# A graph layer with residual and layer norm: normalisation in steps of one block, the first x on another queue, and two planned times

## The chip, the cores and the metric

The kernel runs on one core of a Trainium2 chip. The metric is the device time of one execution in microseconds (us); lower is better. The engines have short names in the profile: PE is TensorE (matrix products), PEld its weight loads, DVE is VectorE, ACT is ScalarE, POOL is GpSimd, SP is SyncE. A name with a q (SPq, ACTq) is the engine's instruction queue, as when it issues a DMA.

## The reference, cut to what matters

There are 6250 nodes with 128 features each, and 100000 edges sorted by their target. Each edge takes the source node's features through one of two linear maps, by its type; the results are summed at the target. A third linear map of the node itself is added, then ReLU, the residual and a layer norm without weights.

```python
Xs = X[src]
m_data = Xs @ W_data.T + b_data
m_ctrl = Xs @ W_control.T + b_control
msg = jnp.where((edge_types == 0)[:, None], m_data, m_ctrl)
agg = jax.ops.segment_sum(msg, dst, num_segments=X.shape[0])
out = agg + (X @ W_self.T + b_self)
...
x = _layernorm(x + relu(out))
```

## The kernel before, in words

The nodes are padded to 49 blocks of 128. The work has two stages.

*Building the messages.* Both maps are linear, so they are applied to the nodes and not to the edges. Step y (L462, L464) multiplies a block of x by W_data and W_control side by side and adds the bias, in float32 in PSUM. The steps yh, y1, ym, y2 and yl cut the result into three bfloat16 parts that add up to it: ACT copies one part out (L473) and PE subtracts it (L480), twice over, and then ACT copies the last. The parts stand in SBUF (m, or m3) and are stored in DRAM as a table. x comes transposed in seven pieces (PARTS: 4 blocks, then 8 at a time) by `load_x`, from ACT's queue. The bias is cut in three in the same way at the very start, by DVE (L271 to L274), and ACT copies its parts into a bfloat16 tile (L276) that the second product of y reads.

*Summing over the edges.* For 35 of the blocks, in seven groups of five, PE fetches the messages by products with 0/1 matrices. While the table is still being built, a group's edges are read in windows (`starts`, one DMA for each block from SP's queue) and sorted into slots (fields, hot, tri, rank, rest, two, v). Where the windows begin is found at the start: r0, one target of every 200 edges, is loaded; DVE compares it (begun, L280); PE counts (L284); POOL fetches one row of edges for each block (er, L290); DVE counts within it; PE turns the result (step "turned", L355); and DVE writes the starts (step "first", L357), which SP reads to issue the windows. Then each block goes through 25 rounds of three steps: g, where PE picks 128 message rows into PSUM (L756, tile g_ps, four buffers); e, where ACT copies them to SBUF as bfloat16 (L771, tile gs, eight buffers; the 25th goes to "mixed"; DVE helps in the last group alone); and s, where PE adds them into the block's sum (L232, agg). Once in a block there is step o: x times W_self and its bias are added to the same sum, with the same helper `by_columns` (L232, agg<-w_sb). The other 14 blocks take their messages from the table by indirect DMAs that POOL issues (msg), and PE sums them (step gm, agg_g).

*Finishing.* When a block's sum is complete, DVE adds its three parts (step whole), adds the residual after the ReLU, and takes mean and variance (step sum). For five blocks together (four in the last, for the final group four and one) `normalise` computes scale and shift (root, rooted, scale), and `apply` has ACT apply them: one instruction of 128x128 at L190 for each block, in place. Then the rows are stored (step out).

*What sets the order.* The order of instructions on each engine is fixed when the program is built, by a planner, `Order`. Each stream of work yields steps with a name, a planned time on an engine, and the steps that it needs. `Order.run` keeps a planned clock for each engine (`free`), and for each step the time at which it can start: when the steps that it needs have ended plus 0.25 us (AFTER). It takes the engine on which something can start first, and among that engine's steps that can start within 0.1 us of that (CLOSE) the one with the smallest due time. The due times are written out in `due`: for a round of block b, 76 + 13.1 x (b + round/25), and 1 more for its copy e; for the normalisation of groups, 76 + 10 + 13.1 x the number of blocks up to the group's end; for y, LEAD plus its block times a pace. Planned times do not change what an instruction does; they decide where it stands in its engine's queue. At run time each engine works its queue in that order, and waits at an instruction whose inputs or buffers are not ready.

Of the kernel before, what the change touches and what calls it, by code (L numbers as in the profile page):

```python
# [9 lines left out]
F32 = mybir.dt.float32  # L10
BF16 = mybir.dt.bfloat16
I32 = mybir.dt.int32
AF = mybir.ActivationFunctionType
# [6 lines left out]
P = 128  # L20
D = 128
D3 = 3 * D
# [86 lines left out]
@with_exitstack  # L109
def kernel(  # L110
    ctx: ExitStack,
    tc: tile.TileContext,
    x: bass.AP,
    xt: bass.AP,
    edges: bass.AP,
    w: bass.AP,
    bias: bass.AP,
    out: bass.AP,
):

    nc = tc.nc  # L140
    dram = ctx.enter_context(tc.tile_pool(name="dram", bufs=1, space=DRAM))
    const = ctx.enter_context(tc.tile_pool(name="const", bufs=1))
    table = dram.tile([NT * P, D3], BF16, name="table")
    packed = dram.tile([NPB, NT * R], BF16, name="packed")
    total = const.tile([1, 1], I32, name="total")

    def finish(h, agg, xs):

        nc.vector.scalar_tensor_tensor(h, agg, 0.0, xs, op0=ALU.max, op1=ALU.add)

    def add_parts(agg, work):
        whole = work.tile([P, D], F32, name="whole")
        nc.vector.tensor_reduce(whole, agg.rearrange("p (i c) -> p c i", i=3), axis=AX.X, op=ALU.add)  # L153
        return whole

    def load_rows(b, work, name="xs", bufs=2):
        xs = work.tile([P, D], F32, name=name, bufs=bufs)
        nc.sync.dma_start(xs, x[b * P : (b + 1) * P, :])
        return xs

    def stats(mv, h, work):
        st = work.tile([P, 6], F32, name="st")
        nc.vector.bn_stats(st, h)
        nc.vector.bn_aggr(mv, st)

    def root(mv, n, work):
        v = work.tile([P, Q], F32, name="v")
        nc.vector.tensor_scalar_add(v[:, :n], mv[:, :n, 1], EPS)
        s0 = work.tile([P, Q], F32, name="s0")
        nc.scalar.activation(s0[:, :n], v[:, :n], AF.Sqrt)  # L170
        return v, s0

    def scale(mv, v, s0, n, work):

        r0 = work.tile([P, Q], F32, name="r0")
        nc.vector.reciprocal(r0[:, :n], s0[:, :n])
        q = work.tile([P, Q], F32, name="q")
        nc.vector.tensor_mul(q[:, :n], v[:, :n], r0[:, :n])
        nc.vector.tensor_add(q[:, :n], q[:, :n], s0[:, :n])
        rstd = work.tile([P, Q], F32, name="rstd")  # L180
        nc.vector.reciprocal(rstd[:, :n], q[:, :n])
        nc.vector.tensor_scalar_mul(rstd[:, :n], rstd[:, :n], 2.0)
        shift = work.tile([P, Q], F32, name="shift")
        nc.vector.scalar_tensor_tensor(shift[:, :n], mv[:, :n, 0], -1.0, rstd[:, :n],
                                       op0=ALU.mult, op1=ALU.mult)
        return rstd, shift

    def apply(h, rstd, shift, n):
        for j in range(n):
            nc.scalar.activation(h[:, j, :], h[:, j, :], AF.Identity,  # L190
                                 bias=shift[:, j : j + 1], scale=rstd[:, j : j + 1])

    def store_out(h, b0, n, by=nc.sync):
        n0 = b0 * P
        full = min(n, (N - n0) // P)
        if full:
            by.dma_start(
                out[n0 : n0 + full * P, :].rearrange("(b p) f -> p b f", p=P), h[:, :full, :]
            )
        if full < n:  # L200
            n1 = n0 + full * P
            nc.sync.dma_start(out[n1:N, :], h[: N - n1, full, :])

    norm = stats, root, scale, apply, store_out

    with ExitStack() as main:
        sums_over_windows(main, tc, x, xt, edges, w, bias, table, packed, total,
                          add_parts, finish, load_rows, norm)

    matched = nc.values_load(total[0:1, 0:1])  # L210
    with tc.If(matched != E), ExitStack() as rest:
        sums_over_all(rest, tc, xt, edges, w, bias, table, dram, finish, load_rows, norm)


def sums_over_windows(ctx, tc, x, xt, edges, w, bias, table, packed, total,
# [21 lines left out]
    early = ctx.enter_context(ExitStack())  # L237
    build = early.enter_context(tc.tile_pool(name="build", bufs=2))
    ps_y = early.enter_context(tc.tile_pool(name="ps_y", bufs=YB, space=PSUM))
    b1 = build.tile([1, D3], F32, name="b1", bufs=1)  # L240
    A.dma_start(b1, bias)
    w_sb = const.tile([D, D3], F32, name="w_sb")
    A.dma_start(w_sb, w)


    iota_f = const.tile([P, 640], F32, name="iota_f")
# [46 lines left out]
        in_offset=bass.IndirectOffsetOnAxis(ap=row_i[:, 0:1], axis=0),  # L293
    )

    order.free.update(V=7.0, T=6.5, G=8.0)


    pid1 = const.tile([P, 1], F32, name="pid1")
# [74 lines left out]
            )  # L374


    xts, ys = {}, {}
    at_part = [sum(PARTS[:g]) for g in range(len(PARTS))]
    two_blocks = [(g, b, min(2, at_part[g] + n - b))
                  for g, n in enumerate(PARTS) for b in range(at_part[g], at_part[g] + n, 2)]  # L380


    LEAD, BUILT = 8.0, 76
    BLOCK = 13.1
    PACE = 1.68
    AHEAD, FIRST = 26.0, 20
# [60 lines left out]
    def load_x():  # L447
        for g, n in enumerate(PARTS):
            free = [("y", at_part[g - 1] - 1)] if g > 1 else []
            yield step(("xt", g), {"A": 0.45}, *free, lag=3.5)  # L450
            xts[g] = build.tile([D, max(PARTS), P], F32, name="xt")[:, :n]
            A.dma_start(xts[g].rearrange("p b c -> p (b c)"),
                        xt[:, at_part[g] * P : (at_part[g] + n) * P])

    def multiply():
        for i, (g, b, n) in enumerate(two_blocks):
            for j in range(n):
                free = [("yl", two_blocks[i - YB][1])] if i >= YB and j == 0 else []
                yield step(("y", b + j), {"T": 0.97}, ("xt", g), *free)
                if j == 0:  # L460
                    y = ys[b] = ps_y.tile([P, 2, 2 * D], F32, name="y")
                T.matmul(y[:, j, :], xts[g][:, b + j - at_part[g], :], w_sb[:, : 2 * D],  # L462
                         start=j == 0, stop=False, skip_group_check=True)
                T.matmul(y[:, j, :], ones_b, bias3[:, : 2 * D], start=False, stop=True, skip_group_check=True)  # L464
# [326 lines left out]
    def own_of(blocks, begun):  # L791

        for i, b in enumerate(blocks):
            yield step(("agg", b), {"S": 0.0}, *([("whole", blocks[i - 1])] if i else []))
            yield step(("o", b), {"T": 0.5}, ("xs", b), begun(b))
            by_columns(aggs[b][:, :D], x_ts.pop(b), w_sb[:, 2 * D :], start=False, stop=False,
                       skip_group_check=True)
            by_columns(aggs[b][:, :D], ones_b, bias3[:, 2 * D :], start=False, stop=False,
                       skip_group_check=True)
# [16 lines left out]
    def normalise(pieces, last):  # L816

        for grp, (get, b0, q0, n) in enumerate(pieces):
            yield step((last, "root", grp), {"V": 0.2}, ("sum", b0 + n - 1))
            h, mv = get()  # L820
            h, mv = h[:, q0 : q0 + n, :], mv[:, q0 : q0 + n, :]
            v, s0 = root(mv, n, work)
            yield step((last, "rooted", grp), {"A": 0.3}, (last, "root", grp))
            yield step((last, "scale", grp), {"V": 1.0}, (last, "rooted", grp))
            scales = scale(mv, v, s0, n, work)
            yield step((last, "apply", grp), {"A": 0.28 * n}, (last, "scale", grp))
            apply(h, *scales, n)
            at_end = last == "p" and grp == len(pieces) - 1
            yield step((last, "out", grp), {"A": 0.4} if at_end else {"S": 0.3}, (last, "apply", grp))
            store_out(h, b0, n, nc.scalar if at_end else nc.sync)  # L830


# [99 lines left out]
def sums_over_all(ctx, tc, xt, edges, w, bias, table, dram, finish, load_rows, norm):  # L932
# [69 lines left out]
    for b0 in range(0, NB, Q):  # L1002
        n = min(Q, NB - b0)
        h = work.tile([P, Q, D], F32, name="h")
        mv = work.tile([P, Q, 2], F32, name="mv")
        for j in range(n):
            s_in = work.tile([P, D], F32, name="s_in")
            nc.sync.dma_start(s_in, sums[(b0 + j) * P : (b0 + j + 1) * P, :])
            xt_b = work.tile([D, P], F32, name="xt_b")
            nc.sync.dma_start(xt_b, xt[:, (b0 + j) * P : (b0 + j + 1) * P])  # L1010
            own = ps.tile([P, D], F32, name="own")
            nc.tensor.matmul(own, xt_b, w_self, start=True, stop=False)
            nc.tensor.matmul(own, one, b_self, start=False, stop=True)
            nc.vector.tensor_add(s_in, s_in, own)
            finish(h[:, j, :], s_in, load_rows(b0 + j, work))
            stats(mv[:, j, :], h[:, j, :], work)
        v, s0 = root(mv, n, work)
        apply(h, *scale(mv, v, s0, n, work), n)
        store_out(h, b0, n)


# [29 lines left out]
```

## Time and profile before

| | |
|---|---|
| median of three timed runs | 545.55 us (544.28 to 546.70) |
| the profiled execution | 628.27 us, span 626.6 us |
| mean granted TensorE clock | 0.985 |
| copies of g_ps to SBUF (L771, ACT) | 804 of 494 ns, 337.2 us busy |
| picking products (L756, PE) | 3430, 330.8 us busy |
| normalising instructions (L190, ACT) | 35 of 497 ns and 14 of 488 ns |
| loads of x for y (L452) | 7 DMAs from ACT's queue, 256 to 512 KB |

The profiled execution is longer than the timed ones, so times read in its trace are compared with its own 628.27 us. A row of the timeline gives the start in us, the length in us, engine, line, operation, out<-in and the count; a row with a count above one merges instructions that follow each other, and its length is from the first start to the last end. What stands in brackets is how long the engine was idle before, and what ended that. A row of the chain of waits gives the start, the length and what the end of the program was then waiting for. Products on PE overlap, so the distance between starts says more than the length of one.

### The profile page before, as it was taken

The page shows a single profiled execution, that of the slowest core. Times are in us where ns is not written, and L with a number is a line of the kernel's source. Part 1 is how long each engine was busy: PE and PEld are TensorE (multiplying, and loading weights), DVE is VectorE, ACT ScalarE, POOL GpSimd, SP SyncE. Part 2 cuts the span into 40 slices and gives each one's busy share as a digit, 9 for nine tenths or more (in the row PEclk, how much of TensorE's full clock was granted, in tenths as well). Part 3 has the DMA queues.
Part 4 walks back from the last instruction along what each step waited for, and adds up shares of the span by engine and source line. Part 5 has one row for each costly group of instructions (what it writes and reads, how often), then busy time and mean ns, then how long its engine had stood idle before and what let it go on. Part 6 is the DMA issues. An engine that isn't in the chain of part 4 may idle for free.

```text
span 626.6 us, 26397 instructions
## 1 busy us (share of the span) xinstructions
PE 550.4 (88%) x11222; PEld 441.2 (70%) x11222; DVE 429.4 (69%) x962; ACT 424.7 (68%) x1008; POOL 292.8 (47%) x267
## 2 busy tenths in 40 slices
PE   5899888896989898897988989999999998888994
PEld 3555466675768686786877877788777787666783
DVE  4767677567667777776787766877686667446784
ACT  6755555565587666777767676786767876676684
POOL 1000026654465556655556464665646554554400
PEclk9999988999899999999999999999999999999998
DMA  3567754324243433435333433443344542534300
GB/s 108 168 196 221 249 188 128 117 66 158 58 127 123 127 111 117 136 109 152 93 128 114 142 122 106 127 144 106 122 133 119 157 152 68 161 103 146 106 18 27
DMA packets 60932, 79.19 MB, mean 126 GB/s; under 512 B 15760, under 2 KB 51371, under 8 KB 60807
## 3 DMA queue, kind: packets, MB, share of 16 engines
q1 hardware_dynamic: 47109, 48.88, 24.3%
q0 software_dynamic: 12400, 25.08, 14.3%
q10 hardware_dynamic: 1298, 3.48, 1.6%
q8 instruction: 89, 1.46, 0.9%
q14 instruction: 36, 0.29, 0.1%
HBM read 64.35 MB, written 13.05 MB: 124 GB/s over the span
## 4 chain that ended last, share of the span: by engine, by line
PE 80%; ACT 7%; issue 5%; DVE 4%; DMA 2%; SPq 1%; another core or an unknown queue 0%; POOL 0%; ACTq 0%; DVEq 0%; POOLq 0%
PE agg L232 27%; PE g_ps L756 26%; PE acc L232 8%; PE agg_g L232 8%; PE small L602 7%; ACT gs L771 5%; PE y L462 2%; ACT h_p L190 1%; DMA rows<-packed 1%; DVE slot L565 1%; PE y L480 1%; DVE hot_st L548 1%; ACT h_g L190 1%; PE y L464 0%; DMA xt<-in_xt 0%
## 5 line engine op out<-in xcount | busy, mean ns | idle before, releaser
L771 ACT CAST gs<-g_ps 128x384 bf16<-128x384 f32 x804 | 337.2, 494 | 151.3 <-PE g_ps L756 97.4
L857 POOL DMA_INDIRECT msg<-table,idx x252 | 283.1, 1124 | 208.0 <-PE g_ps L756 90.5
L756 PE MATMUL g_ps<-m,rows 128*32 128x384 bf16 x3430 | 330.8, 334 | 19.2 <-ACT gs L771 11.6
L232 PE MATMUL agg<-gs,hot_d 128*32 128x384 bf16 x3360 | 304.4, 338 | 27.8 <-ACT gs L771 12.9
L232 PEld LDWEIGHTS <-hot_d 128*32 128x32 bf16 x3500 | 198.9, 137 | 66.7 <-issue 56.4
L756 PEld LDWEIGHTS <-rows 128*32 128x32 bf16 x3430 | 185.5, 138 | 46.4 <-issue 40.6
L565 DVE TENSOR_REDUCE slot<-acc 128x5 bf16<-128x490 f32 x126 | 83.8, 665 | 75.5 <-PE acc L232 39.7
L232 PE MATMUL agg_g<-msg,hot_g 128*32 128x384 bf16 x1008 | 107.2, 330 | 1.2 <-issue 1.1
L741 DVE TENSOR_TENSOR hot_d<-count,to 128x1664 bf16<-128x1664 bf16 x70 | 74.7, 1068 | 21.7 <-PE agg L232 12.8
L602 PE MATMUL small<-hot_st,two 128*32 128x98 bf16 x1260 | 70.9, 290 | 1.4 <-issue 1.3
L602 PEld LDWEIGHTS <-two 128*32 128x32 bf16 x1260 | 56.8, 118 | 6.7 <-issue 4.6
L232 PE MATMUL acc<-hot_st,rest 128*32 128x490 bf16 x476 | 55.1, 380 | 6.1 <-DVE slot L565 5.0
L232 PE MATMUL acc<-hot_st,tri 128*32 128x490 bf16 x504 | 58.8, 376 | 1.0 <-DVE hot_st L548 0.9
L473 ACT CAST m<-y 128x512 bf16<-128x512 f32 (+1 forms) x75 | 40.6, 580 | 25.7 <-PE y L480 18.0
L232 PEld LDWEIGHTS <-hot_g 128*32 128x32 bf16 x1008 | 51.4, 125 | 4.9 <-issue 3.0
L548 DVE TENSOR_TENSOR hot_st<-count,st_b 128x2940 bf16<-128x2940 bf16 x21 | 41.9, 1997 | 13.7 <-PE small L602 5.4
L696 POOL DMA_INDIRECT mixed<-table,row_i x7 | 7.4, 1055 | 87.3 <-PE g_ps L756 81.2
L727 DVE TENSOR_SCALAR rows<-rows,pid 128x3136 bf16<-128x3136 bf16 x35 | 36.3, 1038 | 3.3 <-DMA rows<-packed 3.3
L153 DVE TENSOR_REDUCE whole<-agg 128x128 f32<-128x384 f32 x35 | 19.4, 553 | 27.5 <-PE g_ps L756 23.4
L462 PE MATMUL y<-w_sb,xt 128*128 128x256 f32 x98 | 31.6, 409 | 1.7 <-DMA xt<-in_xt 1.7
L232 PEld LDWEIGHTS <-rest 128*32 128x32 bf16 x476 | 20.9, 99 | 16.0 <-issue 15.3
L771 DVE CAST gs<-g_ps 128x384 bf16<-128x384 f32 x36 | 19.3, 554 | 13.7 <-PE g_ps L756 12.2
(140 smaller groups left out, 423.6 us busy)
## 6 DMA issues: line engine op xcount, KB each, us to landing
rows<-packed SPq DMA_DIRECT2D x35, 784.0 KB
table<-m SPq DMA_DIRECT2D x10, 768.0 KB
msg<-table,idx POOLq DMA_INDIRECT x252
xt<-in_xt ACTq DMA_DIRECT2D x5, 512.0 KB
xt_p<-in_xt SPq DMA_DIRECT2D x35, 64.0 KB
xs_p<-in_x SPq DMA_DIRECT2D x35, 64.0 KB
out<-h_p SPq DMA_DIRECT2D x6, 320.0 KB
table<-m SPq DMA_DIRECT2D x2, 480.0 KB
```

Of the source, the lines that this page charges most:

```text
L153: nc.vector.tensor_reduce(whole, agg.rearrange("p (i c) -> p c i", i=3), axis=AX.X, op=ALU.add)
L232: T.matmul(out[c : c + 32], lhsT[:, c : c + 32], rhs, **flags)
L462: T.matmul(y[:, j, :], xts[g][:, b + j - at_part[g], :], w_sb[:, : 2 * D], start=j == 0, stop=False, skip_group_check=True)
L473: A.copy(part_of(b, n, i), ys[b][:, :n, :].rearrange("p b (t c) -> p t b c", t=2))
L548: V.tensor_tensor(hot, counted[n][:, None, 1 : NT + 1, :].to_broadcast([P, KC, NT, n]), fields[grp][2][:, c * KC : c * KC + KC, None, :].t ...
L565: V.tensor_reduce(slots[grp][:, k, :], by_q, axis=AX.X, op=ALU.max)
L602: T.matmul(vt[c0 : c0 + R, q // 2, :], two[:, k % KC, i, :, q], hot[:, k % KC, :, q], start=k == 0 and q < 2, stop=k == KT - 1, skip_group ...
L727: V.tensor_scalar(rows[b], rows[b], pid1, None, op0=ALU.is_equal)
L741: V.tensor_tensor(hot, counted[DC][:, :, :n], places[grp][:, q, None, c * DC : c * DC + n].to_broadcast([P, P, n]), op=ALU.is_equal)
L756: T.matmul(g_ps[t * R : (t + 1) * R, :D3], rows[b][:, :, s], m3[:, s, :], start=True, stop=True)
L771: (A.copy if e == "A" else V.tensor_copy)(gs[at], g_tiles.pop((b, g))[at, :D3])
L857: G.indirect_dma_start(out=msgs[j, k], out_offset=None, in_=table[:, :], in_offset=bass.IndirectOffsetOnAxis(ap=idx[:, j, k : k + 1], axis=0),
```

## The change

The first load of x (4 blocks, 256 KB) is issued by SP, directly behind r0, in place of ACT. On ACT's queue the weights are now loaded ahead of the bias. The planner's starting clock for PE goes from 6.5 to 5.0 and LEAD, from which the due times of the building steps count, from 8 to 6. `apply` handles one block; in `normalise` each block's application is a planner step of its own of 0.39 us, where there was one step of 0.28 us times the number of blocks. The planned time of y goes from 0.97 to 1.0, that of o (x times W_self) from 0.5 to 0.25. The fallback path for inputs that the windows do not cover calls `apply` in a loop; it is not executed on these inputs.

```diff
-    def apply(h, rstd, shift, n):
-        for j in range(n):
-            nc.scalar.activation(h[:, j, :], h[:, j, :], AF.Identity,
-                                 bias=shift[:, j : j + 1], scale=rstd[:, j : j + 1])
+    def apply(h, rstd, shift, j):
+        nc.scalar.activation(h[:, j, :], h[:, j, :], AF.Identity,
+                             bias=shift[:, j : j + 1], scale=rstd[:, j : j + 1])
...
+    w_sb = const.tile([D, D3], F32, name="w_sb")
+    A.dma_start(w_sb, w)
+    xts = {0: build.tile([D, max(PARTS), P], F32, name="xt")[:, : PARTS[0]]}
+    nc.sync.dma_start(xts[0].rearrange("p b c -> p (b c)"), xt[:, : PARTS[0] * P])
     b1 = build.tile([1, D3], F32, name="b1", bufs=1)
     A.dma_start(b1, bias)
-    w_sb = const.tile([D, D3], F32, name="w_sb")
-    A.dma_start(w_sb, w)
...
-    order.free.update(V=7.0, T=6.5, G=8.0)
+    order.free.update(V=7.0, T=5.0, G=8.0)
...
-    LEAD, BUILT = 8.0, 76
+    LEAD, BUILT = 6.0, 76
...
-            yield step(("xt", g), {"A": 0.45}, *free, lag=3.5)
+            yield step(("xt", g), {"A": 0.45} if g else {"S": 0.0}, *free, lag=3.5 if g else 0.0)
+            if not g:
+                continue
...
-                yield step(("y", b + j), {"T": 0.97}, ("xt", g), *free)
+                yield step(("y", b + j), {"T": 1.0}, ("xt", g), *free)
...
-            yield step(("o", b), {"T": 0.5}, ("xs", b), begun(b))
+            yield step(("o", b), {"T": 0.25}, ("xs", b), begun(b))
...
-            yield step((last, "apply", grp), {"A": 0.28 * n}, (last, "scale", grp))
-            apply(h, *scales, n)
+            for j in range(n):
+                yield step((last, "apply", grp, j), {"A": 0.39}, (last, "scale", grp))
+                apply(h, *scales, j)
             at_end = last == "p" and grp == len(pieces) - 1
-            yield step((last, "out", grp), {"A": 0.4} if at_end else {"S": 0.3}, (last, "apply", grp))
+            yield step((last, "out", grp), {"A": 0.4} if at_end else {"S": 0.3}, (last, "apply", grp, n - 1))
```

More of the change, by code (lines that the diff above doesn't have):

```diff
@@ L374, in starts @@
             )
-    xts, ys = {}, {}
+    ys = {}
     at_part = [sum(PARTS[:g]) for g in range(len(PARTS))]
@@ L1017, in sums_over_all @@
         v, s0 = root(mv, n, work)
-        apply(h, *scale(mv, v, s0, n, work), n)
+        scales = scale(mv, v, s0, n, work)
+        for j in range(n):
+            apply(h, *scales, j)
         store_out(h, b0, n)
```

## The prediction

> **What bounds the kernel now.** I read the page first: the shares of the engines, then the chain that ended last.
>
> ```profile
> PE 550.4 (88%) x11222; PEld 441.2 (70%) x11222; DVE 429.4 (69%) x962; ACT 424.7 (68%) x1008; POOL 292.8 (47%) x267
> PE 80%; ACT 7%; issue 5%; DVE 4%; DMA 2%; SPq 1%; another core or an unknown queue 0%; POOL 0%; ACTq 0%; DVEq 0%; POOLq 0%
> ```
>
> TensorE (PE) is the bound: busy for 88% of the span, on 80% of the chain. ScalarE (ACT) is second, 7% of the chain although it is idle for a third of the time: PE waits for it in places, not on average. So an edit pays only where PE stands still. From the gaps between PE rows of the timeline from 100 to 617 us I count about 51 us of them.
>
> Next the chain of waits, first 20 us, and the timeline there:
>
> ```profile
> 4.16 2.71 DMA xt<-in_xt
> 7.00 1.19 PE y L462 x2
> ```
> ```profile
> 0.83 0.52 ACTq L241 DMA_DIRECT2D b<-in_bias  x1
> 1.38 0.36 ACTq L243 DMA_DIRECT2D w_sb<-in_w  x1
> ...
> 2.24 0.34 DVE L271 CAST parts<-b 1x384 bf16<-1x384 f32 x1
> ...
> 4.30 0.17 DVE L278 CAST r0f<-r 125x4 f32<-125x4 int32 x1 [0.18 <-DMA r<-in_edges]
> ...
> 4.92 0.33 PE L284 MATMUL small<-ones_b,begun 125*49 125x1 bf16 x4 [4.92 <-DVE begun L280]
> ...
> 11.90 0.24 PE L355 MATMUL small<-ident,first_f 49*1 49x49 f32 x2
> ```
>
> The first x is asked for at 4.16, lands 2.71 us later, and PE begins y at 7.00. Also to be seen: VectorE (DVE) cuts the bias in three from 2.24, and only behind that, in its queue, comes r0f at 4.30; PE's row search (L284) hangs on it. At 11.90 PE turns the edge counts, which releases the edge windows.
>
> Then the five normalisations of a group on ACT, in the timeline:
>
> ```profile
> 183.90 2.04 ACT L190 ACTIVATE h_p<-h_p,shift,rstd 128x128 f32<-128x128 f32 x5
> 185.83 2.00 ACT L771 CAST gs<-g_ps 128x384 bf16<-128x384 f32 x5
> 187.96 0.47 ACT L771 CAST mixed<-g_ps 64x384 bf16<-64x384 f32 x1
> ```
> ```profile
> 186.36 0.39 PE L232 MATMUL agg<-gs,hot_d 128*32 128x384 bf16 x4 [1.10 <-issue]
> ```
>
> For about 1.93 us no g_ps is copied out; PE fills its four buffers, then stands for 1.10 us. The same reading at the other seven runs of five (261.68, 289.93, 341.45, 415.30, 470.07, 494.75, 571.76) gives 1.10, 0.83, 0.99, 0.83, 1.32, 0.78, 1.24: in all 8.2 us. The two runs of four near the end cost 0.24 each, since DVE copies too there.
>
> Last, the product with W_self (step o) in PE's timeline:
>
> ```profile
> 610.11 0.45 PE L232 MATMUL agg<-w_sb,xt_p 128*32 128x128 f32 x8
> ...
> 610.33 0.22 PE L232 MATMUL agg<-bias,ones_b 128*32 128x128 bf16 x1
> ...
> 610.39 0.33 PE L232 MATMUL agg<-gs,hot_d 128*32 128x384 bf16 x1
> ```
>
> From its start to the next work is 0.28 us (0.274 at most of the others).
>
> **What the Trainium skill says.** "TensorE: Matmul & The Clock Gate", section on the array of sub-arrays: ACT and DVE are strict first-in-first-out. The trace agrees: five copies stand ready behind the five L190 and go out together at 185.83. The same page, "What's actually happening": a cold array runs at half clock for about 3.4 us of activity. Agrees: y's repeat after 1.07 us until 10.33 and after 0.54 to 0.64 later. "DMA: Bandwidth & Descriptors", "Issuing engines are not separate DMA queues": all queues share the same 16 engines, and another queue saves only issue time. So x gains by being asked for earlier, not by SP.
>
> **The change part by part.**
>
> *Head of the queues.* SP issues r0 from 0.83 to 1.83, then x: issue of about 0.4 (xt rows take 0.33 to 0.45). SP has nothing else before the windows near 12.4, so nobody is late by it. x lands at about 1.85 + 2.71 = 4.6, 2.3 us sooner. ACT's queue loses one xt issue of 0.4 (cover is idle time). But the bias now goes behind w. w's issue is 0.36 and its data moves for about 1 us, so I put the bias 0.5 to 1.0 us later, taking 0.75. That moves the parts chain, r0f, begun and L284 (4.92 to about 5.7), then row_i and POOL's fetch of er (5.94 to 6.7, nothing behind it there), and the counts on DVE (10.03 to 10.8). y stands behind L284 in PE's queue, and its second product needs the bias too: y begins at about 6.0, 1.0 us earlier, not 2.3.
>
> Does the window chain gain? Worked by the rule of Order.run: PE is free at 5.0, "turned" is ready at 11.2 as before (DVE's set, slots and set2 last until 10.05, then 0.6 + 0.3 + 0.25). Before it PE now takes y0 to y5 and three L480 steps; the trace of before has y0 to y4 and one. From 6.0: three cold y of 1.07, three of 0.64, three L480 of 0.2 make 11.7, against 11.90. The 0.75 us of er hide under that. So the windows, thence the rank chain of group 0, move by -0.2 (bounds -0.9 and +0.7), while PE has 1.0 us of y behind it that it need not do later. The first gather at 79.98 stands behind both. I take -0.6, between -1.0 and +0.7.
>
> *Dues.* LEAD 6 in place of 8 stretches the pace of y from 1.22 to 1.27 a block and leaves the last due at 66.7. y at 1.0 for 0.97 adds 1.5 us to the plan over 49 blocks, away from the measured 0.54 to 0.64; it changes places only. Both taken as 0, with 1 us either way.
>
> *Normalisation.* The same 49 L190, the same 0.497 us, no DMA more or less. The plan now takes 5 x 0.39 = 1.95 for a run in place of 1.40; measured spacing is (2.04 - 0.48)/4 = 0.39. Will the run be broken up? Due of group 0's run is 76 + 10 + 13.1 x 5 = 151.5. In the trace five copies and then "mixed", the last of block 5, follow it, so the next copy is number 19, due 76 + 13.1 x (5 + 19/25) + 1 = 152.5: later than 151.5. Each next L190 is at once ready and still due first, so this run stays whole. The same sum leaves the run at 261.68 (seven copies follow before mixed: number 17, due 216.9 against 217.0) one copy between. So mostly the gain is not a break but that the plan knows of 0.55 us more per run and lets PE pull rank, placing or gathered work forward. Bounds: 0 (nothing ready) and 8 x 0.55 = 4.4 less. Such work is ready most of the time (PE does it in every slice), so I take two thirds, -3.0. A break into single L190 would at worst cost each copy behind 0.39, of which the four buffers hide most.
>
> *W_self x.* Same instructions. The plan's 0.5 becomes 0.25 (measured 0.27): 49 x 0.25 = 12 us less planned, and nothing saved by itself. Is PE waiting because of the old value? I count PE gaps in the 0.6 us after each o: 0.3 us over 45 of them, against 2.6 at the mean rate. So PE does not wait there, and the too long value may even be what lets ACT catch up. Bounds -11 and +5.5; taken 0.
>
> Sum: -0.6 - 3.0 = -3.6 us. The profiled execution takes 628.27 us (span 626.6 and 1.7 around it), 15% above the median 545.55 of the timed runs, so its waits may weigh more than theirs; I carry the share over: 624.7/628.27 x 545.55 = 542.4.
>
> **The rivals.**
>
> *Nothing moves (545.5).* The runs stay whole, PE has no other work ready, the copies still dam up for 1.93 us. For it: the due sum above. Against: 8.2 us of gaps at a place that the plan had 0.55 us too short. Range 543.5 to 547.5.
>
> *The plan gets true and PE waits less throughout (538).* If a good half of the 11 us planned too long for o (49 x 0.226) was idle order, 6 us go besides 2.6 of the 3.6: 619.7, which scales to 538. Against: no gaps after o.
>
> *ACT loses its breath (549.8), the slower one.* Copies repeat at 0.385 where the plan has 0.37: over 25 copies of a block ACT falls 0.375 us behind the plan, and o's surplus of 0.226 gives back most of it. Without it, consumers s stand that much sooner behind their copies. If half of 49 x 0.226 = 11 us comes as PE waits for gs, +5.5, and the runs stay whole: 628.27 - 0.6 + 5.5 = 633.2, which scales to 549.8. It decides above 0.06 us a block (3.1 us in all). For it: the almost empty stretch after o. Against: ACT is idle a third of the time and catches up elsewhere.
>
> **How the numbers follow.** Forecast 40% (540 to 544.5), nothing moves 20%, true plan 14%, ACT behind 26%. I count 0.5% (2.7 us) as about what this measurement can tell from no change. Faster: the true plan and 24 of the 40: 38%. Same: 16 of the 40, the 20, 1 of the 26: 37%. Slower 25%. The range 537.5 to 549.5 leaves out a low piece of the third case (about 5 of 14) and half of the last (13 of 26): 18 in 100.
>
> **What would show it.** First y near 6.0 with L284 near 5.7; L355 near 11.7. Runs of L190 still mostly five long, but the PE gap behind them at 0.5 in place of 1.0. Gaps in the 0.6 us after o still near zero; if they reach 3 us or more, the slower rival holds. PE gaps from 100 to 617 near 48 of 51. I am wrong if y begins no earlier, if the runs break up and the gaps vanish whole, or if the new order changes waits in places that no edit names.

## The result, and the profile after

The changed kernel takes 549.63 us (median of 9 runs; 545.48 to 551.40), the kernel before 546.52 (median of 9; 544.28 to 549.21). The ratio is 1.0055 with an interval of 1.0029 to 1.0080: about 3 us slower. (The ratios are worked out from the single runs, so they differ a little from the quotients of the medians.)

By its 628.27 us, the profile shown before the prediction comes from another chip than the timed runs. Two kinds of chip served in this study: on one the kernel before takes 546 to 548 us, on the other 630 to 637, in all its runs and not in the profiled one alone. Every ratio of a run below is taken between kernels on one chip; times are compared within a kind, called the 546 kind and the 630 kind. The profile of the change is of the 546 kind. A profile of the kernel before on that kind, before_3, was made later, and it is the one to hold it against. Line numbers differ by a few between the kernels (L771 of the kernel before is L774 of the change). First lines of both pages, share of the engines and chain, the kernel before first:

```profile
PE 508.0 (93%) x11222; PEld 442.1 (81%) x11222; DVE 427.0 (78%) x962; ACT 420.3 (77%) x1008; POOL 297.5 (54%) x267
PE 71%; DMA 11%; DVE 6%; ACT 5%; issue 3%; SPq 3%; POOL 1%; ACTq 0%; DVEq 0%; POOLq 0%
```
```profile
PE 509.2 (93%) x11222; PEld 441.6 (80%) x11222; DVE 428.4 (78%) x961; ACT 420.1 (76%) x1009; POOL 294.2 (54%) x267
PE 71%; DMA 9%; DVE 9%; ACT 5%; issue 3%; SPq 2%; ACTq 0%; DVEq 0%
```

The work is the same and TensorE (PE) bounds both. The spans are 545.9 and 549.4 us. The head of the queues, in the timeline of the change:

```profile
0.83 0.38 ACTq L240 DMA_DIRECT2D w_sb<-in_w  x1
...
1.24 0.53 ACTq L244 DMA_DIRECT2D b<-in_bias  x1
...
1.89 0.68 SPq L242 DMA_DIRECT2D xt<-in_xt  x1
...
3.30 0.35 DVE L272 CAST parts<-b 1x384 bf16<-1x384 f32 x1 [0.98 <-DMA b<-in_bias]
...
5.73 0.34 PE L285 MATMUL small<-ones_b,begun 125*49 125x1 bf16 x4 [5.73 <-DVE begun L281]
...
5.99 1.22 PE L465 MATMUL y<-w_sb,xt 128*128 128x256 f32 x2
...
12.03 0.24 PE L356 MATMUL small<-ident,first_f 49*1 49x49 f32 x2
```

The bias comes 1.06 us later to DVE (3.30 in place of 2.24), which holds up the row search (L285), and behind it y begins at 5.99 and not when x lands. The edge counts are turned at 12.03 (11.90 in the first profile, 11.77 in before_3). By the first gather the change is still ahead: 78.49 us against 82.02. The loss comes after. The end of block 0's sum stands at 99.3 us against 100.3, that of block 4 at 151.7 against 156.8, that of block 5 at 168.9 against 170.9, and the last product ends at 541.0 against 538.1. So the lead goes from 1.0 us to 5.1 and back to 2.0; from block 8 to 18 the two are within 1 us of each other, and from block 19 on the change is 2 to 3.5 us behind.

Two views say for what PE waits. The groups of instructions from 100 to 545 us (form, count, busy us, mean ns, then the idle time before and what ended it); the kernel before, then the change:

```profile
L232 PE MATMUL agg<-gs,hot_d 128*32 128x384 bf16 x3266 | 288.6, 330 | 5.6 <-ACT gs L771 4.6 <-DVE gs L771 1.0
L232 PE MATMUL agg_g<-msg,hot_g 128*32 128x384 bf16 x996 | 107.3, 330 | 4.5 <-DMA msg<-table,idx 4.3
```
```profile
L231 PE MATMUL agg<-gs,hot_d 128*32 128x384 bf16 x3264 | 290.7, 330 | 6.0 <-ACT gs L774 3.7 <-DVE gs L774 2.1 <-issue 0.2
L231 PE MATMUL agg_g<-msg,hot_g 128*32 128x384 bf16 x996 | 107.8, 331 | 8.3 <-DMA msg<-table,idx 7.9 <-DVE hot_g L873 0.4
```

PE's idle time before the gathered sums (agg_g) grows by 3.8 us, 3.6 of them at gathered messages (msg). Idle time in these rows counts only what is longer than a product's modelled length of 0.33 us. I therefore also count late starts: of every two products of PE that follow each other, from 100 us to the end, how much later the second starts than 0.16 us after the first (0.21 for ranks, placings and y), where it is over by more than 0.01. By this count the kernel before has 27.3 us of late starts, the change 30.5. The 3.2 us more are most of what the change loses in that stretch, 3.9 us from the end of block 0 on; 1.0 of them stand before products that hang on ScalarE's copies, 2.2 before the others.

And the normalisations on ScalarE (ACT), each with the product of PE that stands behind them; the first of the kernel before, then two of the change:

```profile
165.91 2.03 ACT L190 ACTIVATE h_p<-h_p,shift,rstd 128x128 f32<-128x128 f32 x5
...
168.35 0.39 PE L232 MATMUL agg<-gs,hot_d 128*32 128x384 bf16 x4 [0.88 <-ACT gs L771]
```
```profile
163.32 2.08 ACT L189 ACTIVATE h_p<-h_p,shift,rstd 128x128 f32<-128x128 f32 x5
165.26 2.42 ACT L774 CAST gs<-g_ps 128x384 bf16<-128x384 f32 x6
...
298.39 0.53 ACT L189 ACTIVATE h_p<-h_p,shift,rstd 128x128 f32<-128x128 f32 x1
298.79 0.50 ACT L774 CAST gs<-g_ps 128x384 bf16<-128x384 f32 x1
299.15 1.67 ACT L189 ACTIVATE h_p<-h_p,shift,rstd 128x128 f32<-128x128 f32 x4
```
```profile
165.82 0.39 PE L231 MATMUL agg<-gs,hot_d 128*32 128x384 bf16 x4 [1.15 <-ACT gs L774]
...
301.24 0.39 PE L231 MATMUL agg<-gs,hot_d 128*32 128x384 bf16 x4 [0.28 <-ACT gs L774]
```

Six of the eight runs of five are still whole, two have one copy after the first. The gaps of PE behind all normalisations add up to 4.4 us, against 5.6 in the kernel before on the same kind of chip. On the 630 kind they are 4.9 against 8.2; a gap of 2.5 us just before one of the runs in after_2 (482.57 to 485.09) is not in that count.

### The profile page after: what moved, and what is told of

It is laid out like the page before. It is cut to its first block, busy times and chain, and to the rows that moved or that the text cites. A ratio compares the mean times of both kernels' runs of the same rounds, so it can differ in the third digit from the quotient of the medians.

```text
span 549.4 us, 26392 instructions
## 1 busy us (share of the span) xinstructions
PE 509.2 (93%) x11222; PEld 441.6 (80%) x11222; DVE 428.4 (78%) x961; ACT 420.1 (76%) x1009; POOL 294.2 (54%) x267
## 4 chain that ended last, share of the span: by engine, by line
PE 71%; DMA 9%; DVE 9%; ACT 5%; issue 3%; SPq 2%; ACTq 0%; DVEq 0%
PE agg L231 24%; PE g_ps L759 23%; PE acc L231 8%; DMA msg<-table,idx 7%; PE agg_g L231 7%; PE small L605 6%; DVE hot_st L551 2%; ACT gs L774 2%; DVE slot L568 1%; ACT h_p L189 1%; SPq L369 1%; PE y L465 1%; SPq L373 1%; DMA rows<-packed 1%; PE y L483 1%
## 5 line engine op out<-in xcount | busy, mean ns | idle before, releaser
L774 ACT CAST gs<-g_ps 128x384 bf16<-128x384 f32 x803 | 332.6, 497 | 81.8 <-PE g_ps L759 73.2
L759 PE MATMUL g_ps<-m,rows 128*32 128x384 bf16 x3430 | 319.0, 332 | 0.4 <-ACT gs L774 0.2
L231 PE MATMUL agg<-gs,hot_d 128*32 128x384 bf16 x3360 | 300.4, 330 | 6.0 <-ACT gs L774 3.7
L231 PEld LDWEIGHTS <-hot_d 128*32 128x32 bf16 x3500 | 191.8, 137 | 17.6 <-issue 12.0
L231 PE MATMUL agg_g<-msg,hot_g 128*32 128x384 bf16 x1008 | 109.3, 334 | 12.3 <-DMA msg<-table,idx 11.9
L231 PEld LDWEIGHTS <-hot_g 128*32 128x32 bf16 x1008 | 53.0, 124 | 17.1 <-issue 14.5
L231 PE MATMUL acc<-hot_st,tri 128*32 128x490 bf16 x504 | 60.7, 374 | 1.5 <-DVE hot_st L551 1.5
L605 PEld LDWEIGHTS <-two 128*32 128x32 bf16 x1260 | 58.1, 118 | 4.7 <-issue 1.9
L153 DVE TENSOR_REDUCE whole<-agg 128x128 f32<-128x384 f32 x35 | 19.4, 554 | 20.1 <-PE agg L231 16.4
L231 PEld LDWEIGHTS <-rest 128*32 128x32 bf16 x476 | 22.2, 98 | 11.7 <-issue 10.3
L774 DVE CAST gs<-g_ps 128x384 bf16<-128x384 f32 x37 | 20.1, 553 | 6.6 <-PE g_ps L759 3.9
```

The source lines that it names most:

```text
L231: T.matmul(out[c : c + 32], lhsT[:, c : c + 32], rhs, **flags)
L605: T.matmul(vt[c0 : c0 + R, q // 2, :], two[:, k % KC, i, :, q], hot[:, k % KC, :, q], start=k == 0 and q < 2, stop=k == KT - 1, skip_group ...
L759: T.matmul(g_ps[t * R : (t + 1) * R, :D3], rows[b][:, :, s], m3[:, s, :], start=True, stop=True)
L774: (A.copy if e == "A" else V.tensor_copy)(gs[at], g_tiles.pop((b, g))[at, :D3])
```

## The experiments

Letters in the expectations: theory F, the front of the change costs; A, the split normalisation costs; O, the short planned time of o costs; R, any reordering costs or gains about a per cent by chance; S, a surplus in the plan of PE helps; B, ScalarE's planned copy is too short and o's surplus had let it catch up.

**One part alone** (630 kind). b_again is the kernel before unchanged. e_front has the change's lines at the head of the queues, the planner's clock for PE at 5.0 and LEAD 6. e_apply has only the split. e_o is one number:

```diff
-            yield step(("o", b), {"T": 0.5}, ("xs", b), begun(b))
+            yield step(("o", b), {"T": 0.25}, ("xs", b), begun(b))
```

> The kernel before, unchanged, profiled once more. If the 51 us of TensorE gaps of its first profile belong to the kernel, a second profile shows a span near 626 and gaps of 40 to 60 us again. If they belong to that one execution, the span is near 545 and the gaps behind each run of five normalisations shrink from 1.0 to below 0.5 us. Ratio 1.000 within 0.003 either way.

> Only the front of the change: x issued by SP, weights ahead of the bias, planner's TensorE clock 5.0, LEAD 6. Theory F (the front costs it): ratio 1.003 to 1.008. Theory O (the shorter planned time of o costs it) and theory A (the split normalisation costs it): ratio 0.998 to 1.001, with y beginning near 6.0.

> Only the normalisation in steps of one block of 0.39. My prediction: ratio 0.994 to 0.998. Theory A: 1.003 or more. Theories F and O: 0.997 to 1.001.

> Only the planned time of o, 0.25 for 0.5. Theory O (the plan of TensorE runs ahead, so that TensorE meets gathered sums before their messages have landed): ratio 1.003 to 1.010, and 5 us or more of TensorE waiting on DMA msg. Theories F and A: 0.998 to 1.002, and that wait under 2 us.

Measured: b_again 0.999 (0.9968 to 1.0012), span 630.2 and the same gaps as in the first profile, so they belong to the chip. e_front 0.9987 (0.9965 to 1.0008): F falls; y begins at 5.95 and the first gather at 78.0 in place of 81.0, and the lead is gone by block 15. e_apply 1.0043 (1.0023 to 1.0063), where my prediction had a gain. e_o 1.0072 (1.0043 to 1.0101): the largest. PE is idle for 2.3 us before gathered sums there, only 0.3 of them at msg, so that half of O is wrong on this kind of chip.

**The change less one part** (630 kind), with the change and the kernel before again.

> The whole change once more, beside the kernel before on one chip. If the parts add up (front 0.9987, normalisation 1.0043, o 1.0072), the ratio is 1.010. If they share one cause, it stays near 1.0055, between 1.003 and 1.008.

> The kernel before once more. Where it takes about 546 us, TensorE's gaps from 100 us on add up to 15 to 30 us in place of 54, and the copies of g_ps begin 0.43 us after the last start of their products, not 0.9; where it takes about 630 us, both are as in its first two profiles. Ratio 0.997 to 1.003.

> The change without the planned time of o (0.5 kept). Theory O: the loss goes, ratio 0.997 to 1.001, and the wait on DMA msg falls from 12 us to under 4. If any reordering costs about the same (theory R), it stays at 1.003 or more.

> The change without the split of the normalisation. Theory A (the split costs about 0.4%): ratio 1.000 to 1.003. Theory O: still 1.005 or more.

Measured: after_2 1.0069 (1.0049 to 1.0089), before_2 0.9997 (0.9973 to 1.0021). a_no_o 0.9919 (0.9888 to 0.9950): without the new time of o the change would have gained 0.8%, more than I forecast. a_no_apply 1.0159 (1.0115 to 1.0202): taking out the split that costs 0.4% alone makes it 0.9% slower. The parts do not add: front 0.9987 and split 1.0043 make together, with y at 1.0, 0.9919. No run sets y's new time apart, so how much of this is y's and how much interplay stays open.

**The size of the surplus** (546 kind). o at 0.75 and 0.375; then o at 0.25 with the 0.25 us a block given to PE elsewhere, or with ScalarE's copies planned slower:

```diff
-            yield step(("g", b, g), {"T": 0.165}, ("sel", b), *free)
+            yield step(("g", b, g), {"T": 0.17}, ("sel", b), *free)
...
-            yield step(("s", b, g), {"T": 0.165}, ("e", b, g), ("d", b, g // DC), *free)
+            yield step(("s", b, g), {"T": 0.17}, ("e", b, g), ("d", b, g // DC), *free)
```
```diff
-            costs = {"A": 0.37, "V": 0.53} if b >= STARTS[-1] else {"A": 0.37}
+            costs = {"A": 0.39, "V": 0.53} if b >= STARTS[-1] else {"A": 0.39}
```

The first pair is a_pe17, the second a_copy39.

> The change with o planned at 0.75. Theory S (a surplus in the plan of TensorE helps, the more the better): ratio at or below that of the change with 0.5 (0.992), so 0.985 to 0.993. Theory R (any reordering costs or gains about 1% by chance): anywhere from 0.99 to 1.01, no order by size.

> The change with o planned at 0.375, half way. Theory S: half way between 1.007 and 0.992, so 0.997 to 1.002. Theory R: anywhere from 0.99 to 1.01.

> The change with o at 0.25, but each g and each s planned at 0.170 for 0.165: the same 0.25 us a block of surplus, spread over 50 steps. Theory S: the loss goes, ratio 0.990 to 0.997. If it must stand at o itself: 1.004 or more.

> The change with o at 0.25 and each copy of g_ps on ScalarE planned at 0.39 for 0.37, which is where the trace has it (0.371 to 0.385). Theory B (my slower rival: ScalarE falls behind its plan and o's surplus let it catch up): the loss goes, ratio at or below 0.998. If ScalarE's plan is not the cause: 1.004 or more.

Then, on the 546 kind again, o at 0.6 and repeats:

> The kernel before, for a profile on a chip where it takes about 546 us. There, theory S expects TensorE's late starts for copies (steps s and g) at or below the 14 us of the change with o at 0.375, since its surplus is 12 us; theory A expects more than 18 us, behind the runs of five. Where it takes over 620 us, nothing new. Ratio 0.997 to 1.003.

> The change with o kept at 0.5. Theory S: ratio 0.988 to 0.995 on any chip. Theory R: if the 0.992 belonged to one chip, 0.998 or more here.

> The change with o at 0.6, a surplus of 17 us. Theory S with an optimum near 10 us: between the ratio of 0.5 (0.992) and of 0.75 (1.011), so 0.995 to 1.004. Theory R: anywhere from 0.985 to 1.015.

> The change with o at 0.25 and g and s at 0.170. Theory S: 0.988 to 0.995 on any chip. Theory R: 0.998 or more on a chip of another kind.

All on the 546 kind. Surplus is what PE's plan has more than with o at 0.25, over all blocks (49 times the difference in o; 35 x 25 x 2 x 0.005 for a_pe17). Late starts as counted above, those before g and s, which hang on ScalarE's copies, apart from the others (gathered sums, ranks, placings):

| kernel | o | surplus, us | ratio (interval) | late, g and s | late, others |
|---|---|---|---|---|---|
| the change | 0.25 | 0 | 1.0055 (1.0029 to 1.0080) | 18.0 | 12.5 |
| a_copy39 | 0.25 | 0 | 1.0024 (1.0000 to 1.0049) | 15.3 | 11.8 |
| a_o375 | 0.375 | 6 | 0.9974 (0.9946 to 1.0001) | 14.2 | 12.8 |
| a_pe17 | 0.25 | 9 | 0.9912 (0.9880 to 0.9945) | 12.4 | 13.2 |
| a_pe17_2 | 0.25 | 9 | 0.9918 (0.9892 to 0.9945) | 12.6 | 11.8 |
| a_no_o_2 | 0.5 | 12 | 0.9927 (0.9898 to 0.9956) | 12.4 | 12.5 |
| a_o60 | 0.6 | 17 | 0.9996 (0.9966 to 1.0025) | 14.3 | 14.0 |
| a_o75 | 0.75 | 25 | 1.0114 (1.0070 to 1.0159) | 11.9 | 19.4 |

The ratio falls to a surplus of about 10 us and rises beyond. That a_o75 would be the best was expected from S in its simple form, and is wrong. What S forecast for a_o375 and a_pe17 held, and so did the forecast from S with an optimum, 0.995 to 1.004 for a_o60. R gives no reason for an order by size; with so few sizes it is made unlikely, not ruled out. The profiled executions of a_pe17 and a_pe17_2 took 548.1 and 547.1 us, the longest of their runs, so the waits in these two rows do not belong to their median times. At the low end PE stands longer at the copies, at the high end at the rest. The groups of a_no_o_2 and of a_o75, from 100 to 545 us:

```profile
L231 PE MATMUL agg<-gs,hot_d 128*32 128x384 bf16 x3264 | 288.5, 330 | 3.2 <-ACT gs L774 2.4 <-DVE gs L774 0.3
L231 PE MATMUL agg_g<-msg,hot_g 128*32 128x384 bf16 x996 | 107.0, 330 | 6.4 <-DMA msg<-table,idx 6.2
```
```profile
L231 PE MATMUL agg<-gs,hot_d 128*32 128x384 bf16 x3264 | 285.3, 330 | 2.4 <-ACT gs L774 1.2 <-DVE gs L774 1.0
L231 PE MATMUL agg_g<-msg,hot_g 128*32 128x384 bf16 x992 | 104.4, 330 | 12.8 <-DMA msg<-table,idx 12.3 <-DVE hot_g L873 0.4
```

PE's idle time for copies is 6.0 us in the change, 3.2 with o at 0.5, 2.4 at 0.75; for messages 8.3, 6.4 and 12.8. a_pe17 shows that the surplus need not stand at o. a_copy39 lies between what B expected (0.998 or less) and its contrary (1.004 or more): about a quarter of the way from the change to a_no_o_2, with an interval that overlaps the change's. Whether ScalarE's planned time has a part in it stays open. before_3 took 0.9991 (0.9961 to 1.0021), 17.0 us late before g and s and 10.3 otherwise. It has the surplus of o at 0.5 but not the split, the front and y's new time, and S alone had expected 14 at most; so the surplus is not all that sets these waits.

*The granted clock, a rival.* On the 546 kind it does not separate the kernels: the means over the timed runs of each lie between 0.9885 and 0.992, and a_o75, the slowest, has 0.991. On the 630 kind two of the losing kernels were granted less: e_o 0.978 where the kernel before had 0.984 on the same chip, after_2 0.975 against 0.981. Their profiled spans are 5.5 and 7.0 us longer than those of b_again and before_2, but late starts grow by only 1.6 us (92.1 to 93.7) and 0.9 us (94.9 to 95.8). So on that kind most of these two losses is not waiting that the count sees; part can be the clock, and why it was lower no run shows. The gain of a_no_o is waiting: 86.9 us of late starts, 8.0 fewer than in before_2, at a clock of 0.983.

**The split once more** (630 kind).

> Only the normalisation in steps of one block of 0.39, once more. Theory A (the split costs by itself): 1.003 or more, as before. If the split gains by itself what stands behind the runs of five (1 to 3 us): 0.994 to 0.998. If its effect hangs on the rest of the order: between 0.997 and 1.003 here, and a_no_apply_2 on the other side of the change.

> The change without the split, once more. If the split gains by itself: 1.008 or more. Theory A: 1.003 or less. If it hangs on the rest of the order: anywhere from 1.000 to 1.016.

Measured: e_apply_2 1.0058 (1.0034 to 1.0081), a_no_apply_2 1.0123 (1.0085 to 1.0162); the change itself had 1.0069 on this kind. So the split alone costs half a per cent, and within the change it gains as much or more (0.5% and 0.9%; for the first, the change was measured on another chip of that kind). Its effect hangs on the rest of the order. By which placements, no run shows; on the 546 kind it was not run by itself.

## Why the prediction was wrong, by its steps

The forecast was 542.4 and the range 537.5 to 549.5; the time is 549.63.

*The base.* I read 51 us of PE gaps from 100 to 617 us and 8.2 us behind the runs of five as properties of the kernel. On the chips of the timed runs they are 13 and 5.6. I saw that the profiled execution was 15% longer than the timed runs and carried the share over; a difference of that size should have cast doubt on every wait read from it.

*The front.* Right for the row search at 5.7 (5.73) and y at 6.0 (5.99). The bias moved by 1.06 us where I took 0.75, and the turn of the counts, forecast 0.2 us sooner, came 0.1 to 0.3 us later (12.03). The first gather came 3.5 us sooner on the 546 kind and 2.9 in e_front, where I took 0.6; the lead was lost later. In the whole, -0.6 us was forecast, and e_front is at 0.9987, about -0.8 us of 631 and not clear of none.

*The normalisation.* That most runs stay whole is what the trace shows, though the one that was to have a copy between, the second, is whole, and the fourth and fifth are not. That the gap behind them halves is nearly right on the 630 kind (8.2 to 4.9 us, -3.3 where -3.0 was taken) and -1.2 us on the 546 kind. But the saving at that place is not the change of the whole: alone the split costs 0.4 to 0.6%, the other sign than forecast.

*W_self x.* This is the step that failed: "So PE does not wait there, and the too long value may even be what lets ACT catch up. Bounds -11 and +5.5; taken 0." The runs put +1.3% in its place: a_no_o_2 at 0.9927 against the change at 1.0055, about 7 us, past the upper bound, which was 0.9% of the 628 us that it was taken from. On the 630 kind it is 1.5% (0.9919 against 1.0069, on one chip), and 0.7% by itself (e_o), a lower clock included in both. With that term at 7 us the rest of the sum was near: the change without it is 0.8% faster on one kind and 0.7% on the other, where the sum had 0.6%. That is luck in part, since the split, which carried most of that sum, costs by itself. The slower rival had the sign, about the size (+5.5) and the engine: of the 5.6 us by which late starts grow from a_no_o_2 to the change, all stand at g and s (12.4 to 18.0). That its 549.8 is so near 549.63 is luck too: it left out the gain of the rest and took the loss too small. Its place was wrong: the gaps within 0.6 us after o are 0 in the kernel before and 0 in the change (546 kind). The waits are spread over the block. The prediction had named this as a sign of being wrong: waits that change in places that no edit names. Looking only behind o for what its planned time does was the error: a planned time moves all that the planner places after it. That 0.25 is nearer to the measured 0.27 than 0.5 was did not make it the better value.

*The dues.* LEAD was run only together with the rest of the front, in e_front, and y's 0.03 stands in every run made from the change and in none of the others; what they cost stays open.

The version that beats both kernels is the change with o left at 0.5: 544.08 us against 547.54 on the same chip, ratio 0.9927, and 0.9919 on the other kind. a_pe17 is as fast: 543.04 us and ratio 0.9918 in a_pe17_2.

## What to carry to other kernels

In a kernel whose queues are ordered by a list of planned times, a planned time is a control of distance between producers and consumers, and not a measurement to be corrected: vary it in both directions and measure, since a little too long on the bounding engine can be right. Test the parts of such a change in each other's company, because a part that loses alone can win within the whole. And when the profiled execution is 15% longer than the timed ones, get a profile that agrees with the timed runs before adding up waits from it.

## What the runs showed of the hardware

Two kinds of chip ran the same program 15% apart (547.5 and 631 to 637 us), at a mean granted TensorE clock of 0.988 and 0.986 in the profiles. The first gather of the kernel before is at 82.0 us on the one and at 80.0 to 81.4 on the other; all of the difference comes later. On the slower kind, results of PE reach ScalarE later than the records of PE tell: among copies of g_ps that ScalarE was idle for, the median start is 0.43 us after the last start of their products in before_3 and 1.17 us in before_2 (1.19 in the first profile). The length of a copy is nearly the same, 498 and 493 ns. What holds the results up is not in the records, and no run here shows its cause.
